# An addition of the attention's weighted sum moved from VectorE to an accumulating transfer

## The chip, the core and the metric

The kernel runs on one core of a Trainium2 chip. The metric is the device time of one execution in microseconds (us), as the median of several executions. The core has five engines that run side by side: TensorE (PE, matrix products), VectorE (DVE, elementwise work), ScalarE (ACT, activations), GpSimd (POOL, used here almost only to issue transfers) and SyncE (SP, issues transfers). Sixteen DMA engines move the data. Each engine works through its own instructions in order and waits on semaphores for the others.

## The reference, cut to what matters

The network has two residual blocks on 16 images of 1024 channels and 32 x 32 pixels, all in float32. The first block has a local attention over a 3 x 3 neighbourhood in its middle; the second has an ordinary 3 x 3 convolution there.

```python
def self_att(x, ...):                                  # x: 16 x 256 x 32 x 32
    q = relu(bn(conv1x1(x, wq)))
    k = relu(bn(conv1x1(x, wk)))
    v = bn(conv1x1(x, wv))
    kp = unfold3x3(k) + pos                            # 9 neighbours of every pixel
    attn = einsum('bgdhw,bgdkhw->bgkhw', qh, kp)       # 32 heads (g) of 8 channels (d)
    attn = softmax(attn, axis=2)                       # over the 9 neighbours (k)
    v_unf = unfold3x3(v)
    out = einsum('bgdkhw,bgkhw->bgdhw', v_unf, attn)   # the weighted sum over 9 neighbours
    return relu(bn(out))
# block 0: h = relu(bn(conv1x1(x)));  h = self_att(h);  y = relu(bn(conv1x1(h)) + x)
# block 1: three convolutions (1x1, 3x3, 1x1) with norms, plus the residual y, relu
```

The change concerns the last `einsum` of `self_att`: nine products of a weight with a shifted value map, and their sum.

## The kernel before

The 1 x 1 convolutions, and the 3 x 3 convolution in a transformed (Winograd) form, run on TensorE. The attention of an image runs on VectorE: first `logits` (products of q and k, maximum, and on ScalarE the exponentials), then `weighted`. For this the data of an image are laid over 128 partitions as 32 heads times 4 quarters of the image, with 8 channels x 256 pixels = 2048 elements in each partition. The program order is planned in Python: each `yield` hands over an estimate of VectorE's time in us, and a small planner (`Side`) places VectorE's pieces beside TensorE's.

```python
    def relay(what, b):              # loads an image's q, k, positions (or v) into their rooms
        ...
        if what == "qk":
            shapes = (("q", "qc", [HEAD_DIM, JPIX]), ("bnk", "bnk", [HEAD_DIM, HALO]), ("pos", "pc", [NPOS, JPIX]))
        ...
        def move(name, tag, shape):
            t = apool.tile([P] + shape, F32, tag=tag, name=f"{tag}_{b}")     # one room per tag
            nc.gpsimd.dma_start(t.rearrange("p d w -> p (d w)"), backs[name])
        ...
    def make_room(what, b):
        room_for.add((what, b))
        relay(what, b)
    # ... (end of logits)
        def exps():
            for part in parts:
                nc.scalar.activation(part, part, AF.Exp)                     # L628
        yield exps
        make_room("qk", b + 1)
        weights_of[b] = e, tree

    def weighted(b):
        e, tree = weights_of.pop(b)
        vc = projected.pop(b)["bnv"]
        both = ppool.tile([P, 2, HEAD_DIM, JPIX], F32, tag="t", name="acc")
        acc, t = both[:, 0], both[:, 1]

        def term(k, dst):
            i, j = divmod(k, 3)
            nc.vector.tensor_tensor(                                         # L646
                by_row(dst),
                rows(e[:, k, :]).unsqueeze(1).to_broadcast([P, HEAD_DIM, JROWS, W]),
                vc[:, :, i : i + JROWS, j : j + W],
                ALU.mult,
            )
        # ... (last image: a fetch of a kept tile)
        term(0, acc)
        yield 2.3
        for k in range(1, KK):                                               # KK = 9
            if k == FIRST:                                                   # FIRST = 4
                se = apool.tile([P, JPIX], F32, tag="mx", name="se")
                tree(ALU.add, se)                                            # L610 to L613
                nc.vector.reciprocal(se, se)                                 # L661
                yield 4.6
            term(k, t)
            nc.vector.tensor_add(acc, acc, t)                                # L664
            yield 4.6
        nc.vector.tensor_mul(acc, acc, se.unsqueeze(1).to_broadcast([P, HEAD_DIM, JPIX]))   # L666
        summed[b], back = by_quarter("a", b, JPIX, HEAD_DIM)
        nc.sync.dma_start(back, acc.rearrange("p d w -> p (d w)"))           # L668: a<-acc, to DRAM
        make_room("v", b + 1)
        # ...
    # later a<-a (L682) brings the sum back as [channels, pixels], ScalarE applies norm and
    # relu (L690), and the products with a (L405) begin the stage "fused" of this image.
```

The loads of x, s and r tiles (inputs and residuals, L345) and the stores of results (L433) are issued from GpSimd's queue as well. Five buffers hold the loads and four the results.

Of the kernel before, what the change touches and what calls it, by code (L numbers as in the profile page):

```python
# [8 lines left out]
F32 = mybir.dt.float32  # L9
AF = mybir.ActivationFunctionType  # L10
ALU = mybir.AluOpType
AX = mybir.AxisListType

P = 128
# [7 lines left out]
KK = 9  # L22
HEAD_DIM = 8
# [5 lines left out]
JPIX = JROWS * W  # L29
# [43 lines left out]
def sa_bottleneck_kernel(ctx: ExitStack, tc: tile.TileContext, x, w1t, wqkvt, w3t, u1t, u2t, u3t, params, out):  # L73
    nc = tc.nc
# [8 lines left out]
    apool = ctx.enter_context(tc.tile_pool(name="apool", bufs=1))  # L83
    ppool = ctx.enter_context(tc.tile_pool(name="ppool", bufs=2))
# [221 lines left out]
    def rows(ap):  # L306
        return ap.rearrange("p (r w) -> p r w", w=W)
# [145 lines left out]
    def by_quarter(name, b, width, per):  # L453


        t = dram.tile([NJ, NW, P * per // HEAD_DIM, width], F32, tag=f"{name}{b}", name=name)
        return t.rearrange("j n c w -> n c j w"), t.rearrange("j n (g d) w -> (j n g) (d w)", d=per)
# [92 lines left out]
    def relay(what, b):  # L550

        if not ((what, b) in written and (what, b) in room_for):
            return
        moved, backs = projected.setdefault(b, {}), relaid[b]
        if what == "qk":
            shapes = (("q", "qc", [HEAD_DIM, JPIX]), ("bnk", "bnk", [HEAD_DIM, HALO]), ("pos", "pc", [NPOS, JPIX]))
        else:
            shapes = (("bnv", "bnv", [HEAD_DIM, HALO]),)
        def move(name, tag, shape):
            t = apool.tile([P] + shape, F32, tag=tag, name=f"{tag}_{b}")  # L560
            nc.gpsimd.dma_start(t.rearrange("p d w -> p (d w)"), backs[name])
            moved[name] = t.rearrange("p d (r w) -> p d r w", w=PW) if shape[1] == HALO else t
            if len(moved) in (3, 4):
                come[what, b] = max(side.vector, side.tensor) if b else side.tensor

        for i, shape in enumerate(shapes):
            if b < 2 or i == 0:
                move(*shape)
            else:

                moves.append((side.tensor + GAP * i, lambda shape=shape: move(*shape)))
# [5 lines that stand above are left out]
    def by_row(t):  # L577
        return t.rearrange("p d (r w) -> p d r w", w=W)

    def logits(b):  # L580

        qc, kc = (projected[b][name] for name in ("q", "bnk"))
        e = apool.tile([P, KK, JPIX], F32, tag="e", name=f"e_{b}")
        t = ppool.tile([P, 2, HEAD_DIM, JPIX], F32, tag="t", name="prod")
        for k in range(0, KK, 2):
            of = min(2, KK - k)
            for two in range(of):
                i, j = divmod(k + two, 3)
                nc.vector.tensor_tensor(  # L589
                    by_row(t[:, two]), by_row(qc), kc[:, :, i : i + JROWS, j : j + W], ALU.mult  # L590
                )
            yield 2.3 * of
            u = t[:, :of]
            nc.vector.tensor_add(u[:, :, 0:4], u[:, :, 0:4], u[:, :, 4:8])  # L594
            nc.vector.tensor_add(u[:, :, 0:2], u[:, :, 0:2], u[:, :, 2:4])
            nc.vector.tensor_add(e[:, k : k + of, :], u[:, :, 0], u[:, :, 1])
            yield 2.3 * of
        pc = projected[b]["pos"]
        by_tap = e.rearrange("p (i j) n -> p i j n", i=3)
        shape = [P, 2, 3, JPIX]  # L600
        part = by_tap[:, 0:2]
        nc.vector.tensor_tensor(part, part, pc[:, 0:2].unsqueeze(2).to_broadcast(shape), ALU.add)
        shape = [P, 3, 2, JPIX]
        part = by_tap[:, :, 0:2]
        nc.vector.tensor_tensor(part, part, pc[:, 2:4].unsqueeze(1).to_broadcast(shape), ALU.add)
        yield 3.5

        def tree(op, to):
            t = zpool.tile([P, 4, JPIX], F32, tag="z", name="tree")
            nc.vector.tensor_tensor(t, e[:, 0:4, :], e[:, 4:8, :], op)  # L610
            nc.vector.tensor_tensor(t[:, 0:2, :], t[:, 0:2, :], t[:, 2:4, :], op)
            nc.vector.tensor_tensor(to, t[:, 0, :], t[:, 1, :], op)
            nc.vector.tensor_tensor(to, to, e[:, 8, :], op)  # L613

        mx = apool.tile([P, JPIX], F32, tag="mx", name="mx")
        tree(ALU.max, mx)
        yield 2.7

        parts = [e[:, :FIRST], e[:, FIRST:]]
        for part in parts:  # L620
            nc.vector.tensor_tensor(
                part, part, mx.unsqueeze(1).to_broadcast([P, part.shape[1], JPIX]), ALU.subtract
            )
        yield 2.7
# [4 lines that stand above are left out]


        yield exps
        make_room("qk", b + 1)
        weights_of[b] = e, tree

    weights_of = {}
# [1 line left out]
    def weighted(b):  # L637

        e, tree = weights_of.pop(b)
        vc = projected.pop(b)["bnv"]  # L640
        both = ppool.tile([P, 2, HEAD_DIM, JPIX], F32, tag="t", name="acc")
        acc, t = both[:, 0], both[:, 1]

        def term(k, dst):
            i, j = divmod(k, 3)
# [6 lines that stand above are left out]

        if b == B - 1 and DEFERRED and DEFERRED[0] in kept:
            fetch_hidden(DEFERRED[0])
        term(0, acc)
        yield 2.3
        for k in range(1, KK):
            if k == FIRST:
                se = apool.tile([P, JPIX], F32, tag="mx", name="se")
                tree(ALU.add, se)  # L660
                nc.vector.reciprocal(se, se)  # L661
                yield 4.6
            term(k, t)
            nc.vector.tensor_add(acc, acc, t)  # L664
            yield 4.6
        nc.vector.tensor_mul(acc, acc, se.unsqueeze(1).to_broadcast([P, HEAD_DIM, JPIX]))  # L666
        summed[b], back = by_quarter("a", b, JPIX, HEAD_DIM)
        nc.sync.dma_start(back, acc.rearrange("p d w -> p (d w)"))  # L668
        make_room("v", b + 1)
        side.ready[b] = side.vector + 2.3 + RELAY  # L670
        fetch_attended()
        yield 2.3
# [3 lines left out]
    def fetch_attended():  # L676

        b = next_fused[0]
        if b in summed and b not in attended and b not in relu_done:
            a = attended[b] = hpool.tile([P, NW, HW], F32, tag="h", name=f"a_{b}")  # L680
            for n in range(NW):
                nc.sync.dma_start(a[:, n, :].rearrange("p (j w) -> p j w", j=NJ), summed[b][n])  # L682
            side.ready[b] = max(side.ready[b], side.tensor + 8.0)
# [13 lines left out]
    def attend(b):  # L697
        yield from logits(b)
        yield "v"
        yield from weighted(b)  # L700
# [289 lines left out]
    for text in (  # L990
# [5 lines left out]
        for word in text.split():  # L996
            b, _, of = word[1:].partition(":")
# [71 lines left out]
    def fetch_hidden(b):  # L1069
        src = ppool.tile([P, 4 * HW], F32, tag="t", name="hidden")[:, : NW * VROWS * VW]  # L1070
        nc.sync.dma_start(src, kept[b])
        sources[b] = src.rearrange("p (r w) -> p r w", w=VW)
# [340 lines left out]
```

## Time and profile before

The kernel before takes 2402.09 us (median of 3 runs, 2401.06 to 2405.22). The profiled execution has a span of 2397.5 us.

| what | value |
|---|---|
| ScalarE busy | 935.0 us (39%) |
| GpSimd busy | 465.8 us (19%) |
| queue q0 (all transfers from GpSimd) | 118880 packets, 470.87 MB, 54.4% of 16 engines |
| queue q1 (transfers from SyncE and ScalarE) | 175648 packets, 214.49 MB, 28.3% of 16 engines |
| memory traffic | 288 GB/s over the span |

How to read the profile's lines: a group has the line of the kernel, the engine, the operation, `out<-in` by tile names, sizes and the count; then the busy time and the mean length of one in ns; then the idle time of the engine just before the group and what ended most of it. A line of waits has the engine, the tile and line that waited, what it waited for, then the total in us, the number of times and the longest. A line of transfers has the tiles, the issuing queue, the count, the KB of each and the median us from issue to landing.

### The profile page before, as it was taken

What the parts mean: (1) busy time and instruction counts of PE and PEld (TensorE: products, weight loads), DVE (VectorE), ACT (ScalarE), POOL (GpSimd) and SP (SyncE); (2) the same over time, 40 slices, a digit from 0 to 9 for tenths busy, and PEclk for the clock granted to TensorE, in tenths of its full rate; (3) what the DMA queues carried; (4) which work ended last, traced back from release to release, by engine and by line L of the source; (5) the groups of instructions that cost most, each with busy time, mean ns of one, the idle gap of its engine ahead of it and who ended that gap; (6) DMA issues with size and microseconds to landing.
All of it is one profiled execution on the core that took longest, in us unless ns stands there. A gap on an engine that the chain in (4) does not pass through costs nothing.

```text
span 2397.5 us, 18521 instructions
## 1 busy us (share of the span) xinstructions
PE 2365.3 (99%) x6112; PEld 1143.9 (48%) x6112; DVE 2163.7 (90%) x1783; ACT 935.0 (39%) x891; POOL 465.8 (19%) x853
## 2 busy tenths in 40 slices
PE   8999999999999999999999999999999999999998
PEld 3444444444466444444466444444466444444843
DVE  4799998999999999998999999999989999875687
ACT  3323242233222574433122574334222553344278
POOL 3111111111111232111111232111111221111222
PEclk9999999999999999999999999999999999999999
DMA  9969686887798998686888998688788896788977
GB/s 358 350 229 313 241 280 227 258 302 250 287 318 264 322 394 317 225 265 222 260 308 290 306 396 304 233 277 282 251 301 301 308 353 223 255 281 268 331 285 294
DMA packets 295999, 691.05 MB, mean 288 GB/s; under 512 B 20064, under 2 KB 166496, under 8 KB 287456
## 3 DMA queue, kind: packets, MB, share of 16 engines
q0 software_dynamic: 118880, 470.87, 54.4%
q1 hardware_dynamic: 175648, 214.49, 28.3%
q10 hardware_dynamic: 1376, 4.51, 0.5%
q8 instruction: 49, 0.80, 0.1%
q14 instruction: 46, 0.38, 0.0%
HBM read 416.09 MB, written 273.70 MB: 288 GB/s over the span
## 4 chain that ended last, share of the span: by engine, by line
PE 92%; DVE 3%; DMA 3%; ACT 1%; issue 1%; ACTq 0%; SPq 0%; DVEq 0%
PE ps L373 36%; PE ps L405 29%; PE ps L469 13%; PE ps L786 9%; PE ps L1219 4%; PE ps L507 1%; DVE acc L646 1%; DVE acc L664 1%; DMA a<-a 1%; DMA bnk<-kp 1%; DMA U<-uw 0%; DMA uw<-u 0%; DMA V__2_8221<-v 0%; DMA v<-v 0%; DVE form L715 0%
## 5 line engine op out<-in xcount | busy, mean ns | idle before, releaser
L405 PE MATMUL ps<-a,w 128*128 128x512 f32 x1024 | 459.6, 594 | 4.3 <-ACT a L690 4.3
L373 PE MATMUL ps<-result,u 128*128 128x512 f32 x1024 | 459.8, 594 | 3.8 <-ACT result L432 3.8
L373 PE MATMUL ps<-x,w 128*128 128x512 f32 x1024 | 444.4, 595 | 6.4 <-DMA x<-in_x_dram 6.4
L646 DVE TENSOR_TENSOR acc<-e,bnv 128x2048 f32<-128x2048 f32 x144 | 327.6, 2283 | 33.6 <-ACT e L628 30.5
L405 PE MATMUL ps<-y,u 128*128 128x512 f32 x768 | 331.1, 592 | 0.0
L589 DVE TENSOR_TENSOR prod<-qc,bnk 128x2048 f32<-128x2048 f32 x144 | 324.0, 2287 | 1.7
L432 ACT ACTIVATE result<-ps,par 128x1024 f32<-128x1024 f32 x128 | 142.6, 1114 | 463.8 <-PE ps L405 395.4
L373 PEld LDWEIGHTS ps<-x,w 128*128 128x128 f32 x1024 | 195.4, 191 | 252.1 <-issue 251.9
L405 PEld LDWEIGHTS ps<-a,w 128*128 128x128 f32 x1024 | 194.8, 191 | 251.2 <-issue 242.5
L373 PEld LDWEIGHTS ps<-result,u 128*128 128x128 f32 x1024 | 194.8, 190 | 250.7 <-issue 238.2
L664 DVE TENSOR_TENSOR acc<-acc 128x2048 f32<-128x2048 f32 x128 | 293.4, 2292 | 4.4
L405 PEld LDWEIGHTS ps<-y,u 128*128 128x128 f32 x768 | 145.9, 190 | 183.3 <-issue 181.5
L469 PE MATMUL ps<-h,wqk 128*128 128x512 f32 x512 | 222.3, 592 | 0.0
L433 POOL DMA_DIRECT2D r<-result x128 | 68.8, 538 | 633.4 <-ACT result L432 618.0
L594 DVE TENSOR_TENSOR prod<-prod 128x2048 f32<-128x2048 f32 (+1 forms) x80 | 166.2, 2078 | 2.5
L469 PEld LDWEIGHTS ps<-h,wqk 128*128 128x128 f32 x512 | 97.2, 190 | 122.6 <-issue 110.0
L1052 ACT ACTIVATE h<-ps,par 128x1024 f32<-128x1024 f32 x32 | 38.6, 1205 | 280.6 <-PE ps L373 280.6
L432 ACT ACTIVATE result<-ps,bn_sh 128x1024 f32<-128x1024 f32 x96 | 106.6, 1112 | 102.5 <-PE ps L405 102.1
L481 ACT ACTIVATE kp<-ps,par 128x1024 f32<-128x1024 f32 x64 | 77.4, 1210 | 156.5 <-PE ps L469 114.6
L396 ACT ACTIVATE ps<-s 128x1024 f32<-128x1024 f32 x128 | 131.2, 1025 | 2.5
L345 POOL DMA_DIRECT2D x<-in_x_dram x120 | 63.8, 532 | 300.5 <-PE ps L373 229.3
L809 ACT ACTIVATE z<-ps 128x1024 f32<-128x1024 f32 x48 | 49.2, 1025 | 178.1 <-PE ps L786 130.4
(375 smaller groups left out, 2671.4 us busy)
## 6 DMA issues: line engine op xcount, KB each, us to landing
s<-in_x_dram POOLq DMA_DIRECT2D x128, 512.0 KB, 6.2
r<-result POOLq DMA_DIRECT2D x128, 512.0 KB, 4.1
out_dram<-result POOLq DMA_DIRECT2D x126, 512.0 KB, 6.4
x<-in_x_dram POOLq DMA_DIRECT2D x120, 512.0 KB, 5.1
r<-r POOLq DMA_DIRECT2D x111, 512.0 KB, 7.1
v<-v SPq DMA_DIRECT2D x96, 408.0 KB, 4.9
U<-uw SPq DMA_DIRECT2D x72, 512.0 KB, 4.1
bnk<-kp SPq DMA_DIRECT2D x32, 680.0 KB, 7.4
```

Of the source, the lines that this page charges most:

```text
L373: nc.tensor.matmul(ps[n][:, halves(half)], wt[:, c % (NC // 2), n * P : (n + 1) * P], src[:, halves(half)], start=(c == first), stop=(c == ...
L396: nc.scalar.activation(ps, loaded.pop((self.kind, self.b, o)), AF.Identity)
L405: nc.tensor.matmul(self.ahead[o][:, halves(half)], pieces[key][:, n, o % (NC // 2) * P :][:, :P], self.src[:, n, halves(half)], start=Fals ...
L432: nc.scalar.activation(to_, ps, RELU, bias=self.shift(o), scale=1.0)
L469: nc.tensor.matmul(ps[:, halves(half)], pieces[key][:, m, at : at + P], h[:, m, halves(half)], start=(m == 0), stop=(m == NW - 1),)
L481: nc.scalar.activation(dst, src, func, bias=col(f"L0_conv_{name}_b", n), scale=col(f"L0_conv_{name}_s", n),)
L589: nc.vector.tensor_tensor(by_row(t[:, two]), by_row(qc), kc[:, :, i : i + JROWS, j : j + W], ALU.mult)
L594: nc.vector.tensor_add(u[:, :, 0:4], u[:, :, 0:4], u[:, :, 4:8])
L646: nc.vector.tensor_tensor(by_row(dst), rows(e[:, k, :]).unsqueeze(1).to_broadcast([P, HEAD_DIM, JROWS, W]), vc[:, :, i : i + JROWS, j : j ...
L664: nc.vector.tensor_add(acc, acc, t)
L786: nc.tensor.matmul(acc[i][:, at, :, n, :], pieces[key][:, m, at, n * P : (n + 1) * P], v[:, at, :, m * (TILES + TR) :][:, :, :TILES], star ...
L1219: nc.tensor.matmul(ps, w, by, start=i in (1, 2, 7) and not (i == 2 and self.end), stop=True, skip_group_check=True)
```

## The change

The rooms `qc` and `bnk` hold q and k of an image, and are no longer needed once its logits are done. The change puts the first two of the nine products there (`first` and `second`), and lets an accumulating transfer from SBUF to SBUF add `second` onto `first`, while VectorE goes on with the other terms. VectorE adds `first` to the running sum after it has summed the weights. The loads of q and k of the next image, which go into the same rooms, can therefore be released only behind that addition. The purpose is to take one addition of 2048 elements per partition and image off VectorE.

```diff
         yield exps
-        make_room("qk", b + 1)
         weights_of[b] = e, tree
@@ weighted
-        both = ppool.tile([P, 2, HEAD_DIM, JPIX], F32, tag="t", name="acc")
-        acc, t = both[:, 0], both[:, 1]
+        first, second = (
+            apool.tile([P, HEAD_DIM, JPIX], F32, tag=tag, name=name) for tag, name in (("qc", "first"), ("bnk", "second"))
+        )
@@
-        term(0, acc)
+        term(0, first)
         yield 2.3
-        for k in range(1, KK):
+        term(1, second)
+        yield 2.3
+        both = ppool.tile([P, 2, HEAD_DIM, JPIX], F32, tag="t", name="acc")
+        acc, t = both[:, 0], both[:, 1]
+        term(2, acc)
+        yield 2.3
+        nc.gpsimd.dma_start(
+            first.rearrange("p d w -> p (d w)"), second.rearrange("p d w -> p (d w)"), accum_op=ALU.add
+        )
+        for k in range(3, KK):
             if k == FIRST:
                 se = apool.tile([P, JPIX], F32, tag="mx", name="se")
                 tree(ALU.add, se)
                 nc.vector.reciprocal(se, se)
                 yield 4.6
+                nc.vector.tensor_add(acc, acc, first)
+                make_room("qk", b + 1)
+                yield 2.3
             term(k, t)
             nc.vector.tensor_add(acc, acc, t)
             yield 4.6
```

## The prediction

> **What bounds the kernel now.** I read the page's engine shares first, then TensorE's own waits, then the chain of waits near the end.
>
> ```profile
> span 2397.5 us, 18521 instructions
> PE 2365.3 (99%) x6112; PEld 1143.9 (48%) x6112; DVE 2163.7 (90%) x1783; ACT 935.0 (39%) x891; POOL 465.8 (19%) x853
> ...
> L646 DVE TENSOR_TENSOR acc<-e,bnv 128x2048 f32<-128x2048 f32 x144 | 327.6, 2283 | 33.6 <-ACT e L628 30.5
> L664 DVE TENSOR_TENSOR acc<-acc 128x2048 f32<-128x2048 f32 x128 | 293.4, 2292 | 4.4
> ...
> qc<-q POOLq DMA_DIRECT2D x16, 1024.0 KB, 7.4
> a<-acc SPq DMA_DIRECT2D x16, 1024.0 KB, 7.7
> ```
>
> TensorE is busy 2365.3 of 2397.5 us, so all its gaps together are 32.2 us. The timeline shows a group of eight 512-column matmuls every 3.43 us in every full stage, so busy TensorE runs at one steady pace, and the granted clock is 0.998. VectorE is second at 90%; the change works on its row L664, whose additions take 2292 ns each. The view of TensorE's waits says what the 32.2 us are:
>
> ```profile
> PE ps L373 <- DMA x<-in_x_dram: 6.4, 1, 6.4
> PE ps L405 <- ACT a L690: 4.3, 2, 2.9
> PE ps L373 <- ACT result L432: 3.8, 1, 3.8
> PE ps L786 <- issue: 2.3, 1, 2.3
> PE ps L469 <- ACT by_offset L515: 2.2, 1, 2.2
> PE ps L1219 <- ACT result L432: 2.1, 1, 2.1
> ```
>
> With three smaller waits of 2.7 us the list sums to 23.8 us; the other 8.4 us lie after the last matmul. The only wait that VectorE's additions can shorten is the second, 4.3 us, where TensorE waits for the attention result of the last image. The timeline shows it from VectorE's side (bracket: idle time before, and what ended it) and then TensorE's:
>
> ```profile
> 2062.78 4.49 DVE L646 TENSOR_TENSOR acc<-e,bnv 128x2048 f32<-128x2048 f32 x2 [8.71 <-ACT e L628]
> ...
> 2106.58 2.29 DVE L666 TENSOR_TENSOR acc<-acc,se 128x2048 f32<-128x2048 f32 x1
> ```
>
> ```profile
> 2124.36 3.39 PE L405 MATMUL ps<-a,w 128*128 128x512 f32 x4 [2.86 <-ACT a L690]
> 2129.20 5.42 PE L405 MATMUL ps<-a,w 128*128 128x512 f32 x12 [1.45 <-ACT a L690]
> ```
>
> For all other images the result is early: from the end of L666 to the first matmul on it I read, in the timeline, 25.3 us (image 0), 35.7 (1), 46.5 (7), 68.5 (14) and 50 to 270 us for the rest. So VectorE, busy though it is, is not on TensorE's path except at image 15.
>
> [...]
>
> **The change, part by part.**
>
> 1. VectorE. Before, an image has 9 products and 8 additions of 2.29 us. After, terms 0 and 1 go to two tiles of their own, term 2 starts the running sum, terms 3 to 8 add 6 times, and one addition brings in `first`. That is 7 additions: one less, 2.29 us per image, 16 x 2.29 = 36.7 us in all. VectorE falls from 2163.7 to about 2127 us. Nothing else on VectorE changes but its order.
>
> 2. The transfer. It adds 1024 KB of `second` onto 1024 KB of `first`, both in SBUF, 16 times. Estimate of its length: the page gives queue q0 118880 packets, 470.87 MB and 54.4% of 16 engines. 0.544 x 16 x 2397.5 us / 118880 = 175.5 ns for a packet of 3961 bytes, 22.6 bytes per ns and engine. One megabyte over 16 engines is 65536 bytes each, 2.9 us. The plain 1 MB transfers land 7.4 and 7.7 us after issue in the median, traffic included. A second read stream of 2.9 us makes about 10.5 us.
>
> 3. When it must be there. VectorE needs `first` after two more products, one addition, the sum tree and the reciprocal: 3 x 2.29 + 4.6 = 11.5 us from the end of term 1 (4.6 us is what L610 to L661 take in the timeline at 2078.8). The transfer has 11.5 us and I expect about 10.5 in the median, so half the images wait nothing and some wait a few us. I put the average wait at 1 to 2 us, 16 to 30 us in all. So VectorE's net gain in elapsed time is about 10 to 20 us, not 36.7.
>
> 4. GpSimd's queue. The transfer waits there, at the head, for term 1 on VectorE, and the loads of q, k and positions for the next image (moved from before the weighted sum to after the addition of `first`) wait for that addition. I aligned the compiled instruction order of the changed kernel with the times of the kernel before: I took the two neighbouring x, s, r or store issues around each new transfer, and compared their time with the end of term 1, moved up by the work that the new order takes out in front of it. Image 6: neighbours at 859.9 and 860.8 us, term 1 done at 858.1. Image 10: 1384.9 and 1385.8, done at 1384.2. Image 14: 1910.8 and 1914.3, done at 1910.4. Image 15: 2007.1 and 2013.1, done at 2011.2. So the queue would be held up by 0 to 4 us. The load of q sits within 0 to 4 us of the end of its addition as well, if the transfer is in time; a late one is added to this hold-up. The loads stand about 10 us ahead of their use (five buffers, one used every 3.43 us, less 5 to 7 us to landing), so this too stays mostly covered.
>
> 5. Order. Because VectorE is planned 2.3 us shorter per image, some input transforms move behind the weighted sum of image 15. In front of that image's term 1 there is then 56 us less VectorE work than before. Its result comes some 40 us or more earlier even with late transfers, and TensorE's wait of 4.3 us goes away.
>
> 6. TensorE: no instruction added, removed or reordered.
>
> The sum: 2402.1 - 4.3 = 2397.8 us, plus small stalls from part 4 and from shared DMA engines. The worst place for the latter is 835 to 950 us, where the view of stages has the DMA engines at 0.96; images 6, 10 and 14 put their transfer in such a stage. I allow 1 to 2 us in total and predict 2399.
>
> **Rivals.**
>
> (a) A wait takes the place of the one removed: the accumulating transfer is much slower than 10.5 us, say 20 us. Then VectorE waits 8 us per image, 16 x 8 = 130 us, and VectorE has no such room where it counts: of its 2397.5 - 2163.7 = 233.8 us of idle time only 87 lie between 214 and 2050 us in the view of stages, where it is busy 95%. GpSimd's queue is then held 8 us or more at the head, loads lose their 10 us of lead, and TensorE stalls a few us per image: 2410 to 2450. For it: no accumulate was ever timed here[...]. Against it: the author left 11.5 us for it.
>
> (b) VectorE is the hidden bound, and 36.7 us less work shows fully: 2365. Against it: 32.2 us is all the gap TensorE has, 6.4 of it at the first load and 8.4 behind the last matmul, and the results lie ready 25 us or more ahead. I give it next to nothing.
>
> (c) Nothing is seen, because the tail has another bound: after image 15, TensorE waits 0.4, 0.7 and 2.3 us in the transformed convolution at 2220 to 2235, for data that hangs on TensorE's own earlier sums. These move up with TensorE, so the 4.3 should not be given back; if they are, 2402.
>
> **Range and chances.** The lower end is the 4.3 us plus the 3.8 us wait near 330 us, which hangs on a slow copy out of the k halo and can fall either way: 2393. The upper end takes TensorE stalls of about 0.7 us per image: 2412. Faster by over 2% would mean under 2354 us, less than TensorE's busy time: 0.01. Slower by over 2% means over 2450, rival (a) at its worst: 0.04. Within 2%: 0.95.
>
> **What would show it.** VectorE busy near 2127 us with 112 instead of 128 rows of adding `t`, and 16 of adding `first`; the new transfer with 16 issues of 1024 KB and a median near 10.5 us; an idle time before the addition of `first` of 16 to 30 us in all; TensorE busy unchanged at about 2365 us and no wait for `a` at image 15. I am wrong if the transfer's median is over 13 us, if GpSimd's rows show waits for VectorE of over 5 us per image, or if TensorE's waits for x, s or r loads or for `result` grow.

## The result and the profile after

The changed kernel takes 2434.68 us (median, 2433.23 to 2438.71), the kernel before 2401.57 us on the same chip (2399.75 to 2405.22). The ratio is 1.0145, with a 95% interval of 1.013 to 1.0161: about 35 us slower (the two medians differ by 33.1), where 3 us faster had been predicted. The profiled execution has a span of 2437.0 us. It is the longest of the four (2438.71), so the profiles below lie further apart than the medians.

First the page of the changed kernel: span, busy times, and the rows that the change touches.

```profile
span 2437.0 us, 18522 instructions
PE 2379.9 (98%) x6112; PEld 1150.0 (47%) x6112; DVE 2123.9 (87%) x1767; ACT 933.4 (38%) x891; POOL 480.1 (20%) x869
...
L373 PE MATMUL ps<-result,u 128*128 128x512 f32 x1024 | 466.3, 601 | 19.7 <-ACT result L432 19.7
...
L646 DVE TENSOR_TENSOR acc<-e,bnv 128x2048 f32<-128x2048 f32 x112 | 255.1, 2288 | 1.9
L676 DVE TENSOR_TENSOR acc<-acc 128x2048 f32<-128x2048 f32 x96 | 220.0, 2292 | 3.3
```

VectorE has lost its work as planned: 2123.9 us against 2163.7. But the span has grown by 39.5 us (2437.0 - 2397.5), and the whole of it is at TensorE, which has the same 6112 matmuls in the same order. Its idle time is now 2437.0 - 2379.9 = 57.1 us, before 32.2: 24.9 us more. Its busy time is up by 14.6 us, from 2365.3. The view of cores says why: the mean granted clock is 0.991, before 0.998. 0.9% of 2437.0 us is 21.9 us, 0.2% of 2397.5 us is 4.8 us, so by this estimate about 17 us more were taken off the clock. A part of this fell into idle time: in a stretch of 6.83 us at half clock from 1805 us on, shown in the last section, TensorE works for 2.92. The longer matmuls go with the slow clock: set one by one against those of the kernel before, 13.4 of the 14.6 us lie within 0.7 us of a stretch that has a granted clock of 0.50 in one of the two traces. Idle time and longer matmuls together are the loss: 24.9 + 14.6 = 39.5 us.

What TensorE waits for, in the changed kernel (total, times, longest, in us):

```profile
PE ps L373 <- ACT result L432: 19.7, 7, 6.1
PE ps L798 <- DMA U<-uw: 11.2, 4, 7.2
PE ps L373 <- DMA x<-in_x_dram: 6.4, 2, 6.2
PE ps L798 <- ACT z L821: 3.2, 3, 1.6
PE ps L507 <- ACT q L481: 2.5, 1, 2.5
PE ps L405 <- ACT a L702: 2.3, 1, 2.3
```

The wait for the attention result of the last image has shrunk from 4.3 to 2.3 us. In its place the waits for `result` have grown from 3.8 to 19.7 us and those for the transformed weights `U` from 0.4 to 11.2 us. They are not spread over the 16 images. TensorE's timeline of the changed kernel shows four places (start, length, group, and in the bracket the idle time before it and what ended it):

```profile
926.42 6.13 PE L373 MATMUL ps<-result,u 128*128 128x512 f32 x8 [4.51 <-ACT result L432]
932.40 3.60 PE L405 MATMUL ps<-a,w 128*128 128x512 f32 x8
...
1659.04 6.76 PE L373 MATMUL ps<-result,u 128*128 128x512 f32 x8 [3.71 <-ACT result L432]
...
1809.08 5.13 PE L798 MATMUL ps<-V__2_6537,U 128*128 128x256 f32 x16 [7.24 <-DMA U<-uw]
...
1985.13 3.78 PE L373 MATMUL ps<-result,u 128*128 128x512 f32 x4 [6.08 <-ACT result L432]
1989.72 1.98 PE L373 MATMUL ps<-result,u 128*128 128x512 f32 x4 [0.82 <-ACT result L432]
```

The second column matters as much as the bracket. Eight such matmuls take 3.60 us in an undisturbed row of this view, as at 932; after a stall they take 6.13 and 6.76. As the order of the matmuls is the same, the n-th of one trace can be set against the n-th of the other. The four stalls (below called by their times: 926, 1659, 1809, 1985) put TensorE 7.2, 7.1, 8.9 and 10.1 us further behind its own times in the kernel before, slow matmuls included; that is 33 of the 39.5 us.

Last the new transfer. First its landing among other transfers of the changed kernel (count, KB each, median us from issue to landing), then the view of tile `first` (who waited for whom):

```profile
qc<-q POOLq DMA_DIRECT2D x16, 1024.0 KB, 7.6
first<-second POOLq DMA_DIRECT2D x16, 1024.0 KB, 10.8
a<-acc SPq DMA_DIRECT2D x16, 1024.0 KB, 9.2
```

```profile
L663 POOL DMA_DIRECT2D first<-second x16: 886/912/948, 149.6 to 2046.1; - x16
...
  DMA first<-second: 36.1, 12
  DVE second L646: 7.6, 1
...
  POOL qc L561: 77.2, 13
  DVE acc L672: 36.1, 12
```

The transfer is as long as expected. VectorE waits 36.1 us for it, and GpSimd 77.2 us until `first` has been used and the loads of the next image may go.

### The profile page after: what moved, and what is told of

Read it like the earlier page. It is cut to its first block, busy times and chain, and to the rows that moved or that the text cites. A ratio compares the mean times of both kernels' runs of the same rounds, so it can differ in the third digit from the quotient of the medians.

```text
span 2437.0 us, 18522 instructions
## 1 busy us (share of the span) xinstructions
PE 2379.9 (98%) x6112; PEld 1150.0 (47%) x6112; DVE 2123.9 (87%) x1767; ACT 933.4 (38%) x891; POOL 480.1 (20%) x869
## 3 DMA queue, kind: packets, MB, share of 16 engines
q0 software_dynamic: 121184, 487.65, 56.1%
## 5 line engine op out<-in xcount | busy, mean ns | idle before, releaser
L373 PE MATMUL ps<-result,u 128*128 128x512 f32 x1024 | 466.3, 601 | 19.7 <-ACT result L432 19.7
L646 DVE TENSOR_TENSOR acc<-e,bnv 128x2048 f32<-128x2048 f32 x112 | 255.1, 2288 | 1.9
L676 DVE TENSOR_TENSOR acc<-acc 128x2048 f32<-128x2048 f32 x96 | 220.0, 2292 | 3.3
L396 ACT ACTIVATE ps<-r 128x1024 f32<-128x1024 f32 x96 | 97.9, 1021 | 61.6 <-DMA r<-r 54.1
```

What stands on the lines that cost most here:

```text
L373: nc.tensor.matmul(ps[n][:, halves(half)], wt[:, c % (NC // 2), n * P : (n + 1) * P], src[:, halves(half)], start=(c == first), stop=(c == ...
L396: nc.scalar.activation(ps, loaded.pop((self.kind, self.b, o)), AF.Identity)
L646: nc.vector.tensor_tensor(by_row(dst), rows(e[:, k, :]).unsqueeze(1).to_broadcast([P, HEAD_DIM, JROWS, W]), vc[:, :, i : i + JROWS, j : j ...
```

## The experiments

Three theories stood at the beginning, called A, B and C in the expectations. A, transfer: it holds GpSimd's queue and the DMA engines, and that stalls TensorE. B, order: the planner has been told 2.3 us less per image, and so places everything differently; the new order has the stalls. C, late release: the loads of q and k, which now stand in GpSimd's queue behind an addition of VectorE, stall TensorE by themselves. A mixture is possible too. TensorE's order is the same in all kernels of this study. ScalarE's, SyncE's, VectorE's and GpSimd's orders all differ between before and after; "old" and "new order" below mean what the longer and the shorter plan make of them.

All ratios are to the kernel before on the same chip, with the 95% interval. Four combinations of order and transfer come first.

**The transfer left out, the new order kept.** One of the nine terms is missing from the sum.

```diff
-        nc.gpsimd.dma_start(
-            first.rearrange("p d w -> p (d w)"), second.rearrange("p d w -> p (d w)"), accum_op=ALU.add
-        )
```

> The changed kernel without the accumulating transfer (it leaves out the term in `second`); the order on every engine and the late release of q and k stay. Theory A (the transfer: VectorE waits for it, 36 us in the changed kernel, and GpSimd's queue with it, 70 us): 2398 us, TensorE's wait for `result` back to about 4 us. Theory B (the re-planned order, in which steps stand 2.3 us per image earlier on ScalarE, SyncE and GpSimd): about 2425 us or more, with waits of TensorE for `result` near 20 us. Theory C (the late release of q and k in GpSimd's queue by itself): 2410 to 2430, with GpSimd still waiting tens of us for VectorE before the load of q.

Measured: 2408.95 us, ratio 1.0026 (1.0018 to 1.0035). Of the four stalls only 1985 is left (7 us). GpSimd still waits 45.9 us for the addition of `first`. The time lies between what A (2398) and B (2425 or more) expected. So the new order loses something with no transfer at all, and most of the stalls need both.

**The plan as long as before, the transfer kept.**

```diff
                 nc.vector.tensor_add(acc, acc, first)
                 make_room("qk", b + 1)
-                yield 2.3
+                yield 4.6
```

> The changed kernel with 2.3 us more planned after the addition of `first`, so that the plan of an image is as long as before: ScalarE's and SyncE's order are then those of the kernel before, the transfer stays. Theory A (transfer): still slower than before, 2420 to 2435, with VectorE's wait for the transfer near 36 us. Theory B (order): 2395 to 2402. Theory C: 2410 to 2430.

Measured: 2397.99 us, ratio 0.9982 (0.9972 to 0.9992), faster than before. ScalarE's and SyncE's orders are exactly those of before. TensorE's waits and the view of `first` in this kernel:

```profile
PE ps L373 <- DMA x<-in_x_dram: 6.0, 1, 6.0
PE ps L798 <- DMA U<-uw: 4.1, 4, 2.2
PE ps L373 <- ACT result L432: 3.5, 2, 2.1
PE ps L405 <- ACT a L702: 2.3, 1, 2.3
```

```profile
  DMA first<-second: 35.2, 10
  DVE second L646: 7.6, 1
...
  POOL qc L561: 51.5, 11
  DVE acc L672: 35.2, 10
```

This is the decisive run. The transfers are the same 16, VectorE waits as long for them (35.2 against 36.1 us), GpSimd is held for 51.5 us, and TensorE waits 3.5 us for `result` instead of 19.7. It is what B expected; A and C had 2410 us or more. So neither the wait for the transfer nor the late release costs much by itself. The run changes the plan of all engines at once, so it does not say whose order matters. One planned number of 2.3 us, which no engine executes, is worth 1.6% of the time.

**The old order without the transfer**, the fourth corner. It is the kernel above without the transfer (one term missing).

> The kernel whose plan has the 2.3 us back, without the accumulating transfer (one of nine terms is left out of the sum). If the transfer as such costs TensorE nothing where the order is that of before, the ratio is the same as with it, 0.998 within 0.001, and TensorE's waits are the same to 2 us, although VectorE's waits of 35 us for the transfer are gone. If the transfer costs something through the DMA engines or GpSimd's queue there too, the ratio falls to 0.996 or less.

Measured: 2390.21 us, ratio 0.9953 (0.9938 to 0.9967). The expectation of no cost fell: in the old order the transfer costs 0.9982 - 0.9953 = 0.0029, about 7 us (give or take 4, by the two intervals). In the traces it is spread over small waits, such as `result` (1.3 us here, 3.5 with the transfer) and `U` (2.2, with it 4.1), not over one stall.

**The new order without the change**: the kernel before, told 2.3 us less.

```diff
             term(k, t)
             nc.vector.tensor_add(acc, acc, t)
-            yield 4.6
+            yield 4.6 if k > 1 else 2.3
```

> The kernel before with all its 8 additions and no transfer, but with 2.3 us less planned per image, so that ScalarE's and SyncE's order are those of the changed kernel. Theory A: 2398 to 2405. Theory B: 2425 or more. A mixture (order that is too early by what VectorE really takes): 2405 to 2420.

Measured: 2417.7 us, ratio 1.0063 (1.0042 to 1.0085). ScalarE's and SyncE's orders are exactly those of the changed kernel. TensorE waits 11.4 us for `result`; the main stall is the one of 1659 (10 us), which here needs no transfer. A kernel with no transfer and no change in its work becomes slower by the plan alone.

In this table the rows with one addition less also have the late release of q and k.

| VectorE's work | order of before | order of after |
|---|---|---|
| 9 products, 8 additions (before) | 1 | 1.0063 |
| one addition less, no transfer (a term missing) | 0.9953 | 1.0026 |
| one addition less, with the transfer | 0.9982 | 1.0145 |

Down the first column the change behaves nearly as it was meant to. Across, the order costs 0.0063 and 0.0073 without the transfer and 0.0163 with it. The next kernel asks what of the transfer does that.

**A plain copy in place of the accumulating one** (`accum_op` dropped; term 0 is lost from the sum). New order.

> The changed kernel with a plain copy of `second` onto `first` in place of the accumulating one (it leaves out term 0). If the second read stream is what makes the transfer late, its median falls from 10.8 us to about 8, VectorE's wait for it from 36 us to under 10, and theory A gives about 2405 to 2415; theories B and C give 2425 to 2435.

Measured: 2421.43 us, ratio 1.0073 (1.0047 to 1.0099), between the two corners, and between what A and B expected. The copy lands after 8.3 us in the median, against 10.8, and VectorE waits 17.1 us for it.

```profile
L663 POOL DMA_DIRECT2D first<-second x16: 531/531/558, 148.3 to 2034.2; - x16
...
  DMA first<-second: 17.1, 8
```

So what the accumulating transfer has beyond a plain copy costs 0.0072 in the new order. Its later landing (10.8 us against 8.3), its longer packets (the same 121184 packets of queue q0 take 56.1% of 16 engines' span of 2437.0 us, with the copy 54.8% of 2421.7) and its longer issue (912 ns against 531) change together here, and the copy was not run in the old order.

**Other lengths and places in the plan.** Is a plan that is too short the fault (theory D in the expectations), or any other order (F)?

- `yield 4.6 if k > 1 else 6.3` in the kernel before: 1.7 us too long per image.

> The kernel before with 1.7 us more planned per image than VectorE takes; nothing else. ScalarE's and SyncE's orders then differ from those of before by about as many lines as in the changed kernel. Theory D (only a plan that is too early costs): 2398 to 2406. Theory F (the order of before is tuned, and any other order loses): 2412 or more.

Measured: 2445.76 us, ratio 1.018 (1.0151 to 1.0208). Waits for `result` 19.6 us, for `a` 17.3. D expected no loss here.

- Half of the 2.3 us given back: `yield 3.45` behind the addition of `first`.

> The changed kernel with half of the 2.3 us planned back (1.15 us). Theory D, if the loss grows evenly with what is missing in the plan: about 2415. Theory F (order by luck): anything between 2398 and 2435, not tied to the dose.

Measured: 2428.3 us, ratio 1.0102 (1.0087 to 1.0118), with 15.9 us of waits for `z` in the transformed convolution, another stall than any above. Half of the dose does not give half of the loss.

- The addition of `first` and the loads behind it placed before term 6 instead of before term 4, plan short.

```diff
                 yield 4.6
+            if k == 6:
                 nc.vector.tensor_add(acc, acc, first)
```

> The changed kernel with the addition of `first` (and the release of q and k) two terms later, before term 6; the planned length stays 43.7 us, the short one, and nothing is left out. Theory D (what costs is a plan shorter than what VectorE really takes, because it waits for the transfer): the transfer has 9.2 us more, VectorE's wait for it falls from 36 us to near 0, the short plan is then true, and the time is near that of the short plan without transfer, 2403 to 2412. Theory E (the moved order together with the transfer's own traffic): 2420 to 2435.

Measured: 2419.69 us, ratio 1.0073 (1.0056 to 1.009). VectorE's wait for the transfer is gone, but not the loss: TensorE now waits 11.2 us for `a`. This is a third order, so the run shows that a loss does not need that wait, not what the wait costs in the changed kernel; to that speaks the run with the old order, where nearly the same wait stands in a kernel that is faster than before.

- One term later, with 2.3 us planned before it and 2.3 behind it, so that the total is that of before.

> The changed kernel with the addition of `first` one term later (before term 5) and 2.3 us more planned in front of it, so that the plan is as long as before. VectorE waits less than 10 us for the transfer in all, and its plan is true or ahead, but the order on ScalarE and SyncE is another one than before (some 30 lines differ on each). Theory D (a true plan is enough): 2392 to 2398. Theory F: 2403 or more.

Measured: 2422.94 us, ratio 1.0086 (1.0061 to 1.0111), `a` 11.5 us. A theory that only a plan that runs ahead costs time does not survive this row and the first one: too long, and the right total at another place, both lose.

- The 2.3 us planned in front of the addition of `first`, where VectorE waits for the transfer (`yield 6.9` in place of the 4.6 there).

> The changed kernel with 2.3 us more planned, this time in front of the addition of `first`, where VectorE really waits, instead of behind it. ScalarE's and SyncE's order are again those of before. Theory D: 2392 to 2399, and GpSimd's wait for VectorE before the load of q falls from 44 us to about 10, as the load is placed later. If that wait costs TensorE nothing, no faster than with the time behind the addition (2398); if it does, some us faster.

Measured: 2396.64 us, ratio 0.9974 (0.9963 to 0.9986). ScalarE's and SyncE's orders are again exactly those of before. The interval overlaps that of the 2.3 us planned behind the addition (0.9982), so the two places are not told apart.

**The single stalls.** If the loss is a sum of places (theory G in the expectations), each must go with a local edit.

For 1985: ScalarE's timeline of the changed kernel before this stall, then GpSimd's.

```profile
1967.57 1.11 ACT L432 ACTIVATE result<-ps,bn_sh 128x1024 f32<-128x1024 f32 x1 [4.77 <-DMA out_dram<-result]
...
1977.83 1.11 ACT L432 ACTIVATE result<-ps,bn_sh 128x1024 f32<-128x1024 f32 x1 [4.03 <-DMA out_dram<-result]
1983.96 1.11 ACT L432 ACTIVATE result<-ps,par 128x1024 f32<-128x1024 f32 x1 [5.01 <-DMA out_dram<-result]
```

```profile
1954.34 0.53 POOL L561 DMA_DIRECT2D qc<-q  x1 [5.36 <-DVE acc L672]
...
1956.95 0.53 POOL L561 DMA_DIRECT2D bnk<-bnk  x1
...
1964.65 0.53 POOL L561 DMA_DIRECT2D pc<-pos  x1 [4.58 <-DMA qc<-q]
```

ScalarE may not write the next `result` because the store of an earlier one (four buffers) has not landed. q, k and positions of image 15, almost 3 MB, are issued between 1954 and 1965, beside the loads and stores of the running stage; in the order of before they come after it. The edit loads them four terms later, for image 15 alone:

```diff
-                make_room("qk", b + 1)
+                if b + 1 != B - 1:
+                    make_room("qk", b + 1)
                 yield 2.3
+            if k == KK - 1 and b + 1 == B - 1:
+                make_room("qk", b + 1)
             term(k, t)
```

> The changed kernel with the loads of q, k and positions of image 15 released 4 terms later, so that they fall behind the stage U9 of loads and stores at full rate, where the kernel before has them. Theory G: the wait for `result` at 1972 to 1990 us, 7 us and 3 us of slow clock behind it, goes: 2423 to 2428. Theory F: not tied, 2415 to 2450.

Measured: 2425.06 us, ratio 1.0083 (1.0062 to 1.0105). ScalarE's timeline of this kernel at the same place waits for TensorE again, so TensorE is ahead:

```profile
1976.49 1.11 ACT L432 ACTIVATE result<-ps,par 128x1024 f32<-128x1024 f32 x1 [2.37 <-PE ps L405]
...
1980.20 1.11 ACT L432 ACTIVATE result<-ps,par 128x1024 f32<-128x1024 f32 x1 [1.68 <-PE ps L405]
```

TensorE gets back 9.1 us there. The other stalls stay.

For 1809, the transfers in the same stage of three kernels. Changed kernel, 1780 to 1812 us:

```profile
U<-uw SPq DMA_DIRECT2D x5, 512.0 KB, 20.1
...
first<-second POOLq DMA_DIRECT2D x1, 1024.0 KB, 11.0
```

Kernel before, where TensorE is here 19.4 us earlier, 1761 to 1793 us:

```profile
U<-uw SPq DMA_DIRECT2D x8, 512.0 KB, 4.6
```

The loads of `U`, one of which TensorE waits for, take 20.1 us to land in the median. Beside them runs the transfer of image 13, issued at 1785 us. With the old order and the transfer it is issued at 1850, long after TensorE has passed this place (at 1783). So the edit takes this one transfer out (`if b != 13:` in front of it; image 13 lacks one term), and with it VectorE's wait for it, on top of the edit for image 15:

> The kernel with image 15 held, without the accumulating transfer of image 13 alone (it leaves out one term of that image). Where TensorE waits 6.1 us for the transformed convolution near 1804 us, the view of stages has the DMA engines full. Theory G: the transfer of image 13 and its lateness make that stall, it goes, 2416 to 2420. If the loads of q, k and positions of image 14 alone are enough, it stays, 2425.

Measured: 2415.3 us, ratio 1.006 (1.0042 to 1.0079). The interval overlaps that of the edit for image 15 alone, but the trace is clear: set against that kernel, TensorE gains 8.0 us at this place. The same view of this kernel (1780 to 1812 us), and the stretch from 1797 to 1810 us in the view of stages of the changed kernel and of this one (TensorE busy, weight loads, VectorE, ScalarE, GpSimd, granted clock, DMA share, GB/s):

```profile
U<-uw SPq DMA_DIRECT2D x7, 512.0 KB, 7.6
```

```profile
1797.00:1810.00 13.00, 5.76 (x25) 4.77 (x24) 12.35 (x11) 2.05 (x2) 3.17 (x6) 0.81 0.99 370
```

```profile
1797.00:1810.00 13.00, 13.00 (x62) 11.45 (x61) 12.35 (x13) 2.05 (x2) 3.15 (x6) 1.00 1.00 404
```

The DMA share is 0.99 in the row with the stall and 1.00 in the row without it, so the share does not tell the two apart here. What TensorE waits for, 7.24 us, is one particular load of 512 KB.

For 926, where `result` waits for stores as at 1985 (ScalarE 2.18 us in front of the one at 925), there are two candidates: the transfer of image 6, issued at 863 us, and the load of v for image 7, issued at 903 us (in the kernel before at 915). Each was taken away from there alone, both on top of the edit for image 15: the v load moved behind the first products of the next image,

```diff
+            if b == 7 and k == 2:
+                make_room("v", b)
@@ end of weighted
-        make_room("v", b + 1)
+        if b != 6:
+            make_room("v", b + 1)
```

> The kernel with image 15 held (2425 us), and the load of v of image 7 placed four loads later on GpSimd's queue; nothing else moves on any engine. In that kernel TensorE waits 4.6 us for `result` near 928 us and runs 3.1 us behind it at the slow clock. Theory G (too many transfers in a stage that is already full): with 1.36 MB less in the stage this stall shrinks or goes, 2417 to 2422. Theory H (the stall hangs on what stands before it in a queue, not on the bytes): unchanged, 2425.

and the transfer of image 6 left out (one term missing there):

> The kernel with image 15 held, without the accumulating transfer of image 6 alone (it leaves out one term of that image). Theory G: the stall near 928 us (4.6 us and 3.1 of slow clock) goes as in the run without any transfer, 2416 to 2420. If the early load of v does it alone, it stays, 2425.

Measured: 1.0068 (1.0049 to 1.0088) and 1.0067 (1.0044 to 1.009). These intervals overlap that of the edit for image 15 alone, so the ratios do not separate them from it. The traces do: with image 15 held alone TensorE loses 7.7 us near 926, and of these it gains back 4.9 and 5.4. Either of the two takes about two thirds of the stall away, so its full size needs both. (In these two kernels and the one for 1809, ScalarE's, SyncE's and VectorE's orders are those of the edit for image 15 alone; only GpSimd's differs.)

For 1659: in the changed kernel, ScalarE's timeline shows that it stands before the norm of `a`, which the planner has put in front of the next `result`, until `a` has come back from memory:

```profile
1655.33 1.24 ACT L702 ACTIVATE a<-a,par 128x1024 f32<-128x1024 f32 x1 [11.46 <-DMA a<-a]
1656.75 1.24 ACT L702 ACTIVATE a<-a,par 128x1024 f32<-128x1024 f32 x1 [0.18 <-DMA a<-a]
1657.90 1.09 ACT L432 ACTIVATE result<-ps,par 128x1024 f32<-128x1024 f32 x1
```

The edit plans this step later for all images (`side.ready[c] + 8` becomes `+ 14`), and so changes ScalarE's order at many places.

> The changed kernel with one number of the planner raised (8 to 14 us of distance before ScalarE's norm and relu of the attention's result is placed): only ScalarE's order changes, the relu stands a few steps later. In the changed kernel ScalarE waited 11.5 us for `a` at 1655 us in front of a `result` that TensorE needed. Theory G (single places where a step stands in front of what is not ready): the stall there goes, and 7 us with it: 2424 to 2430. Theory F (orders are good or bad as a whole): no such tie, 2415 to 2450.

Measured: 2460.22 us, ratio 1.0237 (1.0216 to 1.0258). That is above what either theory expected. The stall of 1659 is gone, TensorE gains the 7.1 us there, and loses more elsewhere. TensorE's waits of this kernel:

```profile
PE ps L798 <- ACT z L821: 17.2, 6, 11.7
PE ps L405 <- ACT a L702: 16.2, 5, 6.6
PE ps L373 <- ACT result L432: 14.7, 6, 5.6
```

With the edit for image 15 added:

> Both of these edits. Theory G: the gains add up, 2413 to 2420. Theory F: no sum.

Measured: 2447.03 us, ratio 1.0179 (1.0163 to 1.0194): both local gains, and the same new waits, where G had expected 2413 to 2420. A rule changed for all images is no local edit.

**Three of the four at once**: q and k of image 15 later, v of image 7 later, no transfer for image 13.

> The changed kernel with three of its four stalls treated at once: q and k of image 15 loaded four terms later, v of image 7 loaded four loads later, and no transfer for image 13 (one term of that image is left out of the sum). If the loss is a sum of single places, the ratio is that of holding image 15 alone (1.0083) less what the two other edits took out each by itself (0.0015 and 0.0023): 1.0045, a span near 2409 us, with the stall before half of the image at 1655 us still there. If the stalls only move (a rival), the ratio stays at 1.0065 or above.

Measured: 2411.92 us, ratio 1.0036 (1.0022 to 1.005). The expected sum of 1.0045 lies inside the interval, the 1.0083 of image 15 alone far outside. Against the changed kernel's trace TensorE gains 6.0 us near 926, 8.8 at 1809 and 9.1 at 1985, together 23.9, and the span is shorter by 24.7 us; small gains and losses elsewhere nearly cancel. The stall of 1659 is still there (5.8 us). So three local edits take the ratio three quarters of the way back to the kernel before, and the stalls do not just move on.

**Best version.** The one with 6.9 us planned in front of the addition of `first` (0.9974) leaves nothing out and is faster than both kernels: 2396.64 us against 2434.68, and against 2403.9 of the kernel before on the same chip. The gain over before is a quarter of one per cent.

## Why the prediction was wrong

**The step that failed is step 5, "Order".** It said that VectorE is planned 2.3 us shorter per image, counted the work that moves behind image 15 as a gain, and part 1 added "Nothing else on VectorE changes but its order", as if an order were free. Step 6 is true to the letter, TensorE's order did not change, but it was read as "TensorE's times do not change". What TensorE waits for is written by ScalarE (`result`) and loaded by SyncE (`U`), and how soon they could do it here depended on what else was in flight: the loads of `U` at 1809 took 20.1 us to land beside the transfer of image 13, and 7.6 us where that was left out. In the table, going from the old order to the new one costs 0.0163 with the transfer, about 39 us, where the step had zero. The step looked at the 16 new transfers and at image 15; the loss lies in four other places, where transfers, loads, stores or a wait of ScalarE now meet that the old order kept apart. At three of them (926, 1809, 1985) it is the place of GpSimd's transfers and loads: edits there removed the stalls, or two thirds of one, with the other engines' orders left nearly as in the changed kernel. At 1659 it is ScalarE's own order, as far as the trace shows.

**The term that was mis-sized with it** is the allowance of 1 to 2 us for stalls in full stages. The prediction had named the place, 835 to 950 us, with the transfer of image 6 in it. There alone, at 926, TensorE fell back by 7.2 us, and the four stalls together cost 33 us.

**The sum of the old order was good by luck.** Step 5's 2397.8 us without stalls stands beside 2397.99 us measured with the old order, but with two terms that were both too small and cancel. The change without its transfer brings 11 us (0.0047), not 4.3, and the transfer takes back 7 us (0.0029), not 1 to 2. Where the gain comes from is seen in the traces, in which these two kernels are 7.5 us apart. At image 15 TensorE gains 1.9 us. The larger part, 5.8 us, is a wait for `result` near 331 that the prediction had used for its lower end alone. The row of the kernel before, then the same eight matmuls in the kernel before told 2.3 us less:

```profile
330.59 5.40 PE L373 MATMUL ps<-result,u 128*128 128x512 f32 x8 [3.80 <-ACT result L432]
```

```profile
333.28 3.60 PE L373 MATMUL ps<-result,u 128*128 128x512 f32 x8
```

The second kernel saves no addition and the wait is gone all the same, so the saved addition is not needed for this gain; why it goes was not tested.

**The wait for `a` at image 15** fell from 4.3 to 2.3 us, it did not vanish. Step 5 was right that the result comes some 40 us earlier: the sum was ready 15.5 us before TensorE's first matmul on it, in the changed kernel 57.5 us. In the changed kernel's trace ScalarE no longer waits for `a` there; it applies the norm directly behind another `result`, and for that TensorE waits.

**Step 1, VectorE**: 2127 us predicted, 2123.9 measured. Right.

**Step 2, length of the transfer**: 10.5 us predicted, 10.8 measured. Right. Against the plain copy (8.3 us) the adding took 2.5 us more, where the step had put 2.9 us; that a second read stream takes this time was the author's estimate and was not shown. By the packet records of the traces, a packet of 8192 bytes takes 629 ns in the median in the accumulating transfer (2048 packets), and 309 ns in the plain transfers of the kernel before on the same queue (2048 packets), a ratio of 2.0. The whole transfer, from issue to landing, takes 10.8 us against 8.3 of the plain copy, only 1.3 times: so the ratio of the packets does not carry over to the whole.

**Step 3, VectorE's wait**: 16 to 30 us predicted, 36.1 measured, a fifth above the upper end, without weight: in the old order nearly the same wait (35.2 us) stands in a kernel that is faster than before.

**Step 4, GpSimd's queue**: 0 to 4 us per image predicted. 77.2 us over 16 images are 4.8 us, longest 11.8. It was called mostly covered, and with the old order it is (51.5 us held, no large stall). So the length of the hold alone did not decide; the local edits show that it matters which transfers meet in which stage.

**Rival (a)** named the right symptoms, late loads and 2410 to 2450 us, with the wrong cause: the transfer was not slow (10.8 us), and with the old order VectorE waits nearly as long for it in a kernel that is faster than before. **Rival (b)** was rightly given next to nothing: without transfer and in the old order, the kernel with one addition less gains half a per cent. **The conditions for being wrong** worked in part: the growth of TensorE's waits for `result` is the first line of its waits. `U`, with 11.2 us, was not on that list.

**The range** allowed 0.7 us of stall per image, evenly. The stalls came as four of 7 to 10 us. A spread for a kernel with a planned order should have been taken from what another order can do, and 1.0026 to 1.0237 is what the orders other than that of before gave here.

What stays open: why every order that was tried other than that of before loses. That the planner's constants had been tuned around the old one is an obvious guess, but was not tested. The stall of 1659 was not taken away by a local edit either, only by a rule for all images.

## What to carry to other kernels

When a change alters an estimate that places instructions, first build it with the estimate unchanged: then the change and the new order are measured apart. An equal order on the bounding engine does not prove equal times; compare the orders of the engines that feed it, and look in every full stage for the store, load or wait that has moved in. Here the bounding engine was idle for only 32.2 of 2397.5 us, so that a saving elsewhere could bring little, while one megabyte in the wrong stage (the transfer of image 13) cost 8.0 us.

## What the runs showed of the hardware

Each of the four stalls of TensorE cost more than its length: after the stall of 3.71 us at 1659, eight matmuls took 6.76 us instead of 3.60, so that the 3.71 us cost 6.9. In the trace of the changed kernel the granted clock at each of the four places is 0.50 for 6.83 us. These stretches begin at 924.53, 1658.39, 1805.17 and 1982.66 us, which is 2.6, 3.1, 3.3 and 3.6 us after TensorE fell idle. Two of them in the view of stages, at 1659 and at 1809 (columns as above):

```profile
1658.39:1665.22 6.83, 6.18 (x8) 2.56 (x9) 6.73 (x4) 3.69 (x4) 3.17 (x6) 0.50 0.91 320
```

```profile
1805.17:1812.00 6.83, 2.92 (x7) 2.40 (x8) 4.26 (x6) 1.02 (x1) 1.57 (x3) 0.50 1.03 421
```

TensorE works for 6.18 us of the first stretch and for 2.92 us of the second. At half clock half of that is lost, by this estimate 3.1 and 1.5 us. The rows agree: 6.76 us instead of 3.60 behind the stall of 3.71 us, and 5.13 instead of 3.62 behind the longer one of 7.24 us. Together the longer matmuls are 14.6 of the 39.5 us, in a kernel that is 98% busy. Not every wait has such a stretch behind it: after those of 1.58 us at 718 and of 2.28 us at 237 the granted clock stays at 1.00 in the same trace.

The accumulating transfer also takes longer to issue: 912 ns on GpSimd in the median, the plain copy 531.
